# Attention context of a four-layer graph network: products of four heads in 32-column groups with denominators beside them, in place of 64-column products with a denominator column and transposes

## The chip, the cores and the metric

The kernel runs on one NeuronCore of one Trainium2 chip. The metric is the device time of one execution in microseconds (us). Before the change it is 3909.24 us, the median of two runs (3907.55 and 3910.94). Durations of single instructions come from one further execution under the profiler, which took 3906.41 us, with a span of 3904.6 us from its first to its last instruction.

## The reference

The reference takes 32 graphs of 512 nodes, each with 256 features (`x`, 32x512x256, fp32) and an adjacency matrix (`adj`, 32x512x512, int32). Four layers follow each other, and after each its output is added to its input and normalised. Layers 0, 1 and 3 are graph attention layers in which a neighbour's weight comes from two numbers per node. Layer 2 is a transformer layer with 8 heads of 32, and the part of it that matters here is this:

```python
allowed = (adj > 0) | (jnp.swapaxes(adj, 1, 2) > 0) | eye
qkv = x @ Wqkv.T + bqkv
scores = jnp.einsum('bhqd,bhkd->bhqk', q * scale, k)
scores = jnp.where(allowed[:, None], scores, -jnp.inf)
attn = jax.nn.softmax(scores, axis=-1)
ctx = jnp.einsum('bhqk,bhkd->bhqd', attn, v)
ctx = ctx.transpose(0, 2, 1, 3).reshape(B, N, DIM)
attn_out = ctx @ Wo.T + bo
x = _layernorm(x + attn_out, ln1_g, ln1_b)
ff = jax.nn.relu(x @ W1.T + b1) @ W2.T + b2
x = _layernorm(x + ff, ln2_g, ln2_b)
```

For each head, then, a context is a weighted sum of the rows of v, divided by the sum of the weights.

## The kernel before, in words

**Tiling.** A graph's 512 nodes are R = 4 tiles of 128 partitions, its 256 features K = 2 tiles. All work of a graph is in the function `fast_path`; a second function, `general_path`, runs only if a test of the inputs or of the denominators fails (`ok` and `sums` collect what the test needs), which it does not here.

**The order of the work.** `graph(b)` (L723) is a Python generator that writes down one graph's stages: the edge mask, layer 0, layer 1, the symmetric mask, `qkv`, `attention`, the projection (`attended`), `feed forward`, `layer 3`. Each stage is cut into units by `yield`. `paced` gives the unit after its i-th yield a due time, the graph's number times PERIOD plus an entry of the table PLACES, and `heapq.merge` interleaves the units of all 32 graphs by due time. A graph's work is some 430 us long in those units and the period is 120.5, so four graphs are in work at any time: attention of one lies between layer 1 of the next, the feed forward of the one before and so on. TensorE (PE) executes its instructions exactly in this order. The instructions of the other engines are ordered by the framework's scheduler, each in its own queue and in order within it; a helper, `in_place`, ties some of them to the last product before them. A wait of PE therefore holds up everything that is behind it, whichever graph it belongs to.

**PSUM.** There are 8 banks of 128x512 fp32. `bank` (L248) takes one for a product, from a set that depends on the stage: 2 for stages marked "a" (layers 0 and 1), 4 for "b" (qkv, attention, projection), 2 for "c" (feed forward, layer 3).

**qkv (L485).** The features are transposed (`xt2`), and q and k are formed for four heads at a time (qkp). ScalarE (ACT) takes a rounded copy `hi` out of PSUM, VectorE (DVE) the rest `lo`, and DMAs issued by SP spread them into a tile `qk` for two heads, from three buffers. Thus one product with reduced-precision operands gives a score of nearly full precision. v is kept for each node tile with 33 columns for a head: 32 values and a column of ones.

**Attention (L535).** Scores are computed transposed, keys on the partitions. For a pair of heads hp and a tile j of 128 keys there are two products s (128x512), two exponentials on ACT (L553, without subtraction of a maximum), and for j = 0 to 2 one multiplication by the mask on DVE (L556). For j = 3 the mask is instead added in PSUM by a second product with `shut`. When all four j of a pair are done, eight products `cp` follow, of 64 columns of v for each head: 32 values, the ones, and 31 columns of no interest. The two heads of a pair use the two halves of the array's columns and of one PSUM bank. ACT copies the bank to `cs` (L572). These eight products, of two instructions each because they are fp32, are one unit.

**Projection (L576).** The contexts stand with features on the partitions, but each head's denominator stands on one partition only. So for each node tile r four transposes (ctp<-cs) bring the nodes onto the partitions, a reciprocal (L587) and a multiplication (L591) divide, and eight further transposes (ctp<-ctx, in `transposed`, L306) turn the result back into `ct`, features on the partitions, as the product with Wo (wop) needs it.

What a PE unit is called later: s scores, cp context products, ctp context transposes, wop projection, f1p and f2p feed forward, o products of layers 0, 1 and 3, h0p, h1p, h3p their projections, gp a row of node numbers spread over partitions, xt0p to xt3p and ytp transposes.

Of the kernel before, what the change touches and what calls it, by code (L numbers as in the profile page):

```python
# [9 lines left out]
F32 = mybir.dt.float32  # L10
BF16 = mybir.dt.bfloat16
# [17 lines left out]
    "edges": [-1440, -1440, -410, 1420],  # L29
    "x": [3260],  # L30
    "mask": [16220, 16520, 16600, 17520],
    "layer 0": [
        2410, 3594, 4534, 4534, 5073, 5753, 5753, 5823, 6123, 6123, 6233, 6233, 6603, 6773, 6903,
        7687, 7687, 7777, 8077, 8077, 8157, 8287, 8439, 8439,
    ],
    "layer 1": [11037, 11066, 11277, 11729, 11849, 11879, 12043, 13286, 13554, 14195, 14884],
    "qkv": [17180, 17740, 18270, 18270, 18270, 18990, 19484, 19654, 21635, 21635],
    "attention": [
        20262, 20932, 21922, 21982, 22092, 22092, 22092, 22350, 22350, 23077, 23537, 23537,
        24028, 24208, 24328, 24532, 25064, 25220, 25368, 25943,  # L40
    ],
    "projection": [26801, 26801, 26861, 26911, 27661, 27721, 28721, 29140, 29256, 29848],
    "feed forward": [
        31013, 31120, 32042, 32263, 32263, 32465, 32710, 33771, 33983, 34076, 34284, 34691,
        35070, 35329, 35615, 36103, 36646, 37299,
    ],
    "layer 3": [39714, 39714, 40906, 41226, 41406, 41526, 41526, 42359, 42359, 42379, 42379],
# [6 lines left out]
RD_MAX = 1e25  # L54
# [18 lines left out]
def fast_path(ctx: ExitStack, tc: tile.TileContext, a: dict, out: bass.AP, bad: bass.AP):  # L73
# [21 lines left out]
    VC = DH + 1  # L95
    ND = R * (H + 2 + H2)
# [33 lines left out]
    sums = const.tile([P, 2, 2 * B], F32, name="sums")  # L130

# [4 lines left out]
    v = const.tile([P, R, H2 * VC + 2 * DH - VC], F32, name="v")  # L136
    nc.gpsimd.memset(v, 1.0)
# [110 lines left out]
    def bank(name, dtype=F32):  # L248
        shape = [P, 2048 // (2 if dtype == BF16 else 4)]
        n = 4 if stage[0] == "b" else 2  # L250
        return ps.tile(shape, dtype, tag="mm" + stage[0], name=name, bufs=n)

    def part(name):

        return buf([P, N], "part", name, {"a": 7, "b": 6, "c": 5}[stage[0]])
# [229 lines left out]
    def qkv(x):  # L485
# [31 lines left out]
        for r in range(R):  # L517
            yield
            p = bank("vp")
            for k in range(K):  # L520
# [7 lines left out]
            nc.scalar.copy(  # L528
                v[:, r, : H2 * VC].rearrange("p (h e) -> p h e", h=H2)[:, :, :DH],
                p[:, :D].rearrange("p (h e) -> p h e", h=H2),  # L530
            )
# [3 lines left out]
    def attention(qk, a2, shut):  # L535
        cs = []
        for hp in range(H2 // 2):
            pr = []
            for j in range(R):
                yield  # L540
                t = sb.tile([P, 2, N], F32, tag="pr", name="pr", bufs=4)
                for i in range(2):
                    s = bank("s")
                    product(nc.tensor.matmul,
                    s,
                        qk[hp][:, 1, i, j * P : (j + 1) * P],
                        qk[hp][:, 0, i, :],
                        start=True,
                        stop=j < R - 1,
                    )  # L550
                    if j == R - 1:
                        product(nc.tensor.matmul, s, identb, shut, start=False, stop=True)
                    nc.scalar.activation(t[:, i, :], s, AF.Exp, scale=QSCALE)  # L553
                if j < R - 1:
                    edges = a2[:, j, :].unsqueeze(1).to_broadcast([P, 2, N])
                    nc.vector.tensor_mul(t, t, edges)  # L556
                pr.append(t)

            yield
            cp = bank("cp")  # L560
            for j in range(R):
                for i in range(2):
                    first = (2 * hp + i) * VC
                    product(nc.tensor.matmul,
                    cp[i * 2 * DH : (i + 1) * 2 * DH, :],
                        v[:, j, first : first + 2 * DH],
                        pr[j][:, i, :],
                        start=j == 0,
                        stop=j == R - 1,
                    )  # L570
            t = part("cs")
            nc.scalar.copy(t, cp)  # L572
            cs.append(t)
        return cs

    def attended(x, cs, rd):  # L576
        ctx_ = []
        for r in range(R):
            yield
            p = bank("ctp")  # L580
            for hp in range(H2 // 2):
                product(nc.tensor.transpose,
                    p[:, hp * P : (hp + 1) * P], cs[hp][:, r * P : (r + 1) * P], ident
                )
            o = p.rearrange("p (h e) -> p h e", h=H2)
            rdr = rd[:, r * H2 : (r + 1) * H2].unsqueeze(2)
            nc.vector.reciprocal(rdr, o[:, :, DH : DH + 1])  # L587
            if r % 2 == 0:
                t = part("ctx").rearrange("p (r d) -> p r d", d=D)
            ctx_.append(t[:, r % 2, :])  # L590
            nc.vector.tensor_mul(  # L591
                ctx_[r].rearrange("p (h e) -> p h e", h=H2),
                o[:, :, :DH],
                rdr.to_broadcast([P, H2, DH]),
            )
# [805 lines left out]
```

## Time and profile before

| What | Value |
|---|---|
| median of the runs | 3909.24 us |
| the profiled execution | 3906.41 us |
| its span, first to last instruction | 3904.6 us |
| PE, matmuls: busy | 3753.3 us, 96% |
| DVE: busy | 2674.8 us, 69% |
| ACT: busy | 1926.2 us, 49% |
| GpSimd (POOL): busy | 346.9 us, 9% |
| DMA, main queue | 257.71 MB, 23.1% of 16 engines |
| mean granted TensorE clock | 0.983 |

In the lines of the profile, `L102 PE MATMUL cp<-pr,v 128*64 128x512 f32 x2048 | 474.9, 600 | 17.8 <-DVE ...` says: source line, engine, operation, tile written and tiles read, the array's rows and columns used, shape and type, count; then the busy time in us that is put down to the group and the mean of one in ns; then the idle time of the engine just before such instructions and what ended it. All products go through the helper `product`, so they all have line 102 and are told apart by their tiles. PEld is the weight load that goes with every matmul. Matmuls are pipelined, and their ends are modelled, so that durations overlap: the distance from one start to the next is the price of a matmul. In a timeline the first two columns are the start and the length of a run of like instructions. In a list of waits the columns after the colon are the total in us, the number of waits and the longest.

### The profile page before, as it was taken

The numbers are of one execution on the slowest core, as the hardware profiler recorded it, in microseconds if no ns is written. First come the engines' busy times: TensorE is split into PE (matmuls) and PEld (weight loads), VectorE is DVE, ScalarE is ACT, GpSimd is POOL, SyncE is SP. The second block draws the span as 40 slices with busy tenths as digits, with TensorE's granted clock in tenths as the row PEclk, the third lists the DMA queues.
The fourth block names the chain that finished last, engine by engine and source line by source line (L and its number), as shares of the span: only waits on it lengthen the run. The fifth ranks groups of instructions, "written<-read, shape, count | busy, mean of one in ns | idle before, by whom it ended". The sixth has DMA issues, their size and how long they took to land.

```text
span 3904.6 us, 53602 instructions
## 1 busy us (share of the span) xinstructions
PE 3753.3 (96%) x19238; PEld 2824.5 (72%) x19238; DVE 2674.8 (69%) x5594; ACT 1926.2 (49%) x4257; POOL 346.9 (9%) x266
## 2 busy tenths in 40 slices
PE   5899999999999999999999999999999999999996
PEld 4577777777777777777777777777777777777764
DVE  4667676677677677677677677677777677777653
ACT  2444455444455544455544455545555544555442
POOL 0000010000010001010001010001010001010000
PEclk6899999999999999999999999999999999999998
DMA  3222222222222222222222222222222222221120
GB/s 106 77 73 65 72 58 67 71 76 67 70 60 65 71 76 69 68 62 63 71 76 71 66 63 64 69 76 71 66 65 65 65 76 74 63 67 58 49 54 12
DMA packets 180431, 261.20 MB, mean 67 GB/s; under 512 B 36800, under 2 KB 72768, under 8 KB 180160
## 3 DMA queue, kind: packets, MB, share of 16 engines
q1 hardware_dynamic: 180160, 257.71, 23.1%
q8 instruction: 155, 2.54, 0.3%
q14 instruction: 116, 0.95, 0.1%
HBM read 106.57 MB, written 16.78 MB: 32 GB/s over the span
## 4 chain that ended last, share of the span: by engine, by line
PE 60%; DVE 14%; issue 8%; ACT 5%; POOL 5%; POOLq 0%; ACTq 0%
PE o L102 16%; PE f1p L102 7%; PE f2p L102 6%; PE qkp L102 5%; PE cp L102 5%; DVE pr L556 4%; ACT y L275 4%; POOL rs L270 3%; PE h3p L102 3%; PE s L102 3%; PE h1p L102 3%; PE wop L102 3%; POOL st L297 2%; PE gp L102 2%; PE vp L102 2%
## 5 line engine op out<-in xcount | busy, mean ns | idle before, releaser
L556 DVE TENSOR_TENSOR pr<-pr,a 128x1024 f32<-128x1024 f32 x384 | 459.1, 1216 | 319.3 <-ACT pr L553 319.2
L275 ACT ACTIVATE y<-y,rs 128x256 f32<-128x256 f32 x768 | 398.4, 589 | 438.2 <-DVE rs L271 438.2
L393 DVE SCALAR_TENSOR_TENSOR pt<-gb,ex,at 128x512 f32<-128x512 f32 x768 | 530.6, 744 | 77.6 <-ACT gb L345 77.6
L553 ACT ACTIVATE pr<-s 128x512 f32<-128x512 f32 x1024 | 545.2, 613 | 7.4 <-PE s L102 7.3
L102 PEld LDWEIGHTS o<-hv,pt 128*128 128x128 f32 x4096 | 508.4, 199 | 23.7 <-issue 8.4
L102 PE MATMUL o<-hv,pt 128*128 128x65 f32 x4096 | 502.7, 280 | 9.7 <-DVE pt L393 9.7
L102 PE MATMUL f2p<-wf,ft 128*128 128x256 f32 x2048 | 491.6, 383 | 12.3 <-ACT ft L638 12.2
L102 PE MATMUL cp<-pr,v 128*64 128x512 f32 x2048 | 474.9, 600 | 17.8 <-DVE pr L556 17.1
L102 PE MATMUL f1p<-yt,wf 128*128 128x256 f32 x2048 | 488.9, 381 | 0.3 <-DVE yt L302 0.3
L102 PE MATMUL o<-h,pt 128*128 128x257 f32 x2048 | 482.8, 383 | 3.7 <-DVE pt L393 3.7
L102 PEld LDWEIGHTS o<-h,pt 128*128 128x128 f32 x2048 | 381.5, 190 | 96.0 <-issue 40.6
L270 POOL TENSOR_TENSOR rs<-rs,mhalf 128x4 f32<-128x4 f32 x192 | 246.2, 1282 | 2118.8 <-DVE rs L269 1826.0
L638 ACT ACTIVATE ft<-f1p,cols 128x256 f32<-128x256 f32 x512 | 215.2, 474 | 442.2 <-PE f1p L102 442.2
L102 PEld LDWEIGHTS f2p<-wf,ft 128*128 128x128 f32 x2048 | 380.1, 191 | 69.5 <-ACT ft L638 17.1
L102 PEld LDWEIGHTS f1p<-yt,wf 128*128 128x128 f32 x2048 | 385.3, 191 | 54.5 <-DVE yt L302 0.8
L102 PE MATMUL s<-qk 128*128 128x512 f32 x1024 | 395.1, 481 | 1.6 <-ACT pr L553 1.6
L102 PEld LDWEIGHTS cp<-pr,v 128*64 128x64 f32 x2048 | 133.0, 136 | 286.0 <-issue 194.2
L266 DVE BATCH_NORM_STATS2 bn<-y 128x6 f32<-128x256 f32 x768 | 294.6, 411 | 4.5
L102 PEld LDWEIGHTS s<-qk 128*128 128x128 f32 x1024 | 187.8, 190 | 99.3 <-issue 40.6
L102 PE MATMUL qkp<-xt,wqkv 128*128 128x512 f32 x512 | 231.3, 594 | 0.0
L345 ACT COPY gb<-gp 128x512 f32<-128x512 f32 x192 | 111.5, 581 | 219.4 <-PE gp L102 219.4
L428 DVE RECIPROCAL rd<-o 128x4 f32<-128x4 f32 x128 | 23.4, 183 | 272.7 <-PE o L102 272.7
(134 smaller groups left out, 4582.5 us busy)
## 6 DMA issues: line engine op xcount, KB each, us to landing
qk<-hi SPq DMA_DIRECT2D x1024, 64.0 KB, 2.0
qk<-lo SPq DMA_DIRECT2D x1024, 64.0 KB, 2.0
adjt<-in_adjt SPq DMA_DIRECT2D x64, 512.0 KB, 3.5
adj<-in_adj SPq DMA_DIRECT2D x64, 512.0 KB, 3.6
xt<-in_xt SPq DMA_DIRECT2D x32, 512.0 KB, 3.4
x<-in_x SPq DMA_DIRECT2D x32, 512.0 KB, 4.7
out<-y SPq DMA_DIRECT2D x32, 512.0 KB, 3.0
wf<-in_w1t SPq DMA_DIRECT2D x1, 1024.0 KB, 7.6
```

The lines of the kernel that those rows point to most:

```text
L102: latest[0] = what(*args, **kwargs).ins.name
L266: nc.vector.bn_stats(st[:, r, :], y[:, r, :])
L270: nc.gpsimd.tensor_tensor(rs[:, 1, :], rs[:, 0, :], mhalf[:, :R], op=ALU.pow)
L275: nc.scalar.activation(y[:, r, :], y[:, r, :], AF.Identity, bias=rs[:, 2, r : r + 1], scale=rs[:, 1, r : r + 1],)
L297: nc.gpsimd.tensor_tensor(st[:, 2, :], st[:, 1, :], mhalf[:, :G], op=ALU.pow)
L345: nc.scalar.copy(g, p)
L393: nc.vector.scalar_tensor_tensor(t, g, f, edges, op0=ALU.max, op1=ALU.mult)
L428: nc.vector.reciprocal(rdh, o[:, :, HO:])
L553: nc.scalar.activation(t[:, i, :], s, AF.Exp, scale=QSCALE)
L556: nc.vector.tensor_mul(t, t, edges)
L638: nc.scalar.activation(ft[:, f, :], p[:, f, :], AF.Relu, bias=bf1[:, ff + f : ff + f + 1])
```

## The change

Layer 2's context products are arranged anew.

Attention now works on halves of the heads (c = 0 and 1, four heads each). For each tile j of keys the two pairs' scores, exponentials and masks come first, and then one unit of eight products: four `cp`, of 32 columns of v for each of the four heads, into one PSUM bank, each head in its own quarter of the array's columns and of the partitions; and four `dp`, the same with a constant 128x32 tile of ones in place of v, into another bank. So every partition of a head holds that head's denominator. The two banks accumulate over the four j, and there are two such banks in all (tag acc).

At the end of a half, DVE forms the reciprocal of dp (128x512) and multiplies cp by it straight into `ct`, which has the features on the partitions already. Two sums on ACT for each half (over dp and over rec) feed the test at the end of the kernel in place of the small reciprocals that `ok` held before. The copies `cs`, all ctp transposes, the small reciprocals, the divisions and the copies out of PSUM into `ct` are gone. v has 32 columns a head, and is copied flat.

Further: the products of stages a and b share one set of four banks; there are five buffers for probabilities in place of four, and two of the tag part in stage b in place of six; and the table PLACES has new due times for all stages, with the same period. The end of the kernel has some more instructions on small tiles.

```diff
-    VC = DH + 1
-    ND = R * (H + 2 + H2)
+    ND = R * (H + 2)
...
-    sums = const.tile([P, 2, 2 * B], F32, name="sums")
+    sums = const.tile([P, 4, 2 * B], F32, name="sums")
...
-    v = const.tile([P, R, H2 * VC + 2 * DH - VC], F32, name="v")
-    nc.gpsimd.memset(v, 1.0)
+    v = const.tile([P, R, D], F32, name="v")
+    ones = const.tile([P, DH], F32, name="ones")
+    nc.gpsimd.memset(ones, 1.0)
...
-        n = 4 if stage[0] == "b" else 2
-        return ps.tile(shape, dtype, tag="mm" + stage[0], name=name, bufs=n)
+        tag, n = ("c", 2) if stage[0] == "c" else ("ab", 4)
+        return ps.tile(shape, dtype, tag="mm" + tag, name=name, bufs=n)
...
-            nc.scalar.copy(
-                v[:, r, : H2 * VC].rearrange("p (h e) -> p h e", h=H2)[:, :, :DH],
-                p[:, :D].rearrange("p (h e) -> p h e", h=H2),
-            )
+            nc.scalar.copy(v[:, r, :], p[:, :D])
...
-    def attention(qk, a2, shut):
-        cs = []
-        for hp in range(H2 // 2):
-            pr = []
+    def attention(b, qk, a2, shut):
+        ct = sb.tile([P, K, N], F32, tag="ct", name="ct", bufs=1)
+        for c in range(K):
+            acc = [ps.tile([P, N], F32, tag="acc", name=n, bufs=2) for n in ("cp", "dp")]
             for j in range(R):
+                pr = []
+                for hp in range(2):
+                    yield
+                    t = sb.tile([P, 2, N], F32, tag="pr", name="pr", bufs=5)
+                    for i in range(2):
+                        s = bank("s")
+                        product(nc.tensor.matmul,
+                            s,
+                            qk[2 * c + hp][:, 1, i, j * P : (j + 1) * P],
+                            qk[2 * c + hp][:, 0, i, :],
+                            start=True,
+                            stop=j < R - 1,
+                        )
+                        if j == R - 1:
+                            product(nc.tensor.matmul, s, identb, shut, start=False, stop=True)
+                        nc.scalar.activation(t[:, i, :], s, AF.Exp, scale=QSCALE)
+                    if j < R - 1:
+                        edges = a2[:, j, :].unsqueeze(1).to_broadcast([P, 2, N])
+                        nc.vector.tensor_mul(t, t, edges)
+                    pr += [t[:, 0, :], t[:, 1, :]]
                 yield
...
-            yield
-            cp = bank("cp")
-            for j in range(R):
-                for i in range(2):
-                    first = (2 * hp + i) * VC
-                    product(nc.tensor.matmul,
-                    cp[i * 2 * DH : (i + 1) * 2 * DH, :],
-                        v[:, j, first : first + 2 * DH],
-                        pr[j][:, i, :],
-                        start=j == 0,
-                        stop=j == R - 1,
-                    )
-            t = part("cs")
-            nc.scalar.copy(t, cp)
-            cs.append(t)
-        return cs
+                for o, p in enumerate(acc):
+                    for i in range(4):
+                        first = (4 * c + i) * DH
+                        product(nc.tensor.matmul,
+                            p[i * DH : (i + 1) * DH, :],
+                            ones if o else v[:, j, first : first + DH],
+                            pr[i],
+                            start=j == 0,
+                            stop=j == R - 1,
+                        )
+            rec = part("rec")
+            nc.vector.reciprocal(rec, acc[1])
+            nc.vector.tensor_mul(ct[:, c, :], acc[0], rec)
+            for o, t in enumerate((acc[1], rec)):
+                junk = sb.tile([P, N], BF16, tag="junk", name="junk", bufs=1)
+                i = 2 * b + c
+                nc.scalar.activation(junk, t, AF.Copy, accum_out=sums[:, 2 + o, i : i + 1])
+        return ct
...
-            p = bank("ctp")
-            for hp in range(H2 // 2):
-                product(nc.tensor.transpose,
-                    p[:, hp * P : (hp + 1) * P], cs[hp][:, r * P : (r + 1) * P], ident
-                )
...
-            nc.vector.reciprocal(rdr, o[:, :, DH : DH + 1])
...
-        ct = yield from transposed(ctx_, "ct")
```

Of PLACES, the rows that touch attention (in hundredths of a us, by the table's own clock):

```diff
     "attention": [
-        20262, 20932, 21922, 21982, 22092, 22092, 22092, 22350, 22350, 23077, 23537, 23537,
-        24028, 24208, 24328, 24532, 25064, 25220, 25368, 25943,
+        20222, 20892, 22312, 22312, 22312, 22702, 22702, 22702, 23260, 23260, 23260, 23837,
+        24057, 24127, 24502, 24502, 24502, 24872, 25302, 25444, 26080, 26580, 26580, 26880,
     ],
-    "projection": [26801, 26801, 26861, 26911, 27661, 27721, 28721, 29140, 29256, 29848],
+    "projection": [29111, 29590, 29906, 29928],
```

## The prediction

> **What bounds the kernel now.** I read the page's busy shares first, then the busy times of two neighbouring stretches in the middle of the run, then what TensorE waited for there, then the groups, then the timeline around the lines that change. The page:
>
> ```profile
> PE 3753.3 (96%) x19238; PEld 2824.5 (72%) x19238; DVE 2674.8 (69%) x5594; ACT 1926.2 (49%) x4257; POOL 346.9 (9%) x266
> PE   5899999999999999999999999999999999999996
> ```
>
> TensorE is full from the third slice to the last but one. A busy PE is a modelled figure, so I look at the rhythm. The chain in order of time has the layer 3 transposes (xt3p x5) at 1952.60 and again at 2069.35 us: one graph every 116.75 us. Two stretches of that length, by engine (PE, PEld, DVE, ACT, POOL):
>
> ```profile
> 2000.00:2116.78 116.78, 115.09 (x602) 86.99 (x601) 83.12 (x175) 60.01 (x133) 10.75 (x8) 1.00 0.24 68
> 2116.78:2233.56 116.78, 115.08 (x602) 86.98 (x601) 83.11 (x175) 60.01 (x133) 10.76 (x8) 1.00 0.24 68
> ```
>
> They are alike to 0.01 us: a steady state at full clock, in which TensorE is idle for 116.78 - 115.09 = 1.69 us. What it waits for, over 20 graphs (1000 to 3336 us):
>
> ```profile
> PE gp L102 <- ACT ex L665: 14.1, 20, 0.7
> PE cp L102 <- DVE pr L556: 9.9, 20, 0.5
> PE xt3p L102 <- ACT y L275: 9.8, 60, 0.2
> ```
>
> These are 0.70, 0.49 and 0.49 us for each graph, the whole 1.69. So the period is the sum of what TensorE is given, and a microsecond per graph, taken or added, is about 32 us of the total. The groups that change:
>
> ```profile
> L102 PE MATMUL cp<-pr,v 128*64 128x512 f32 x2048 | 474.9, 600 | 17.8 <-DVE pr L556 17.1 <-DVE mv L267 0.6
> L102 PE MATMUL ctp<-ident,cs 128*128 128x128 f32 x512 | 67.2, 279 | 2.7 <-ACT cs L572 2.7
> L102 PE MATMUL ctp<-ident,ctx 128*128 128x128 f32 x256 | 39.5, 280 | 0.0
> L591 DVE TENSOR_TENSOR ctx<-ctp,rd 128x256 f32<-128x256 f32 x128 | 48.4, 418 | 0.0
> L587 DVE RECIPROCAL rd<-ctp 128x8 f32<-128x8 f32 x128 | 17.7, 178 | 0.0
> ```
>
> The means of PE overlap, so I take prices from starts. One visit of the context products (16 instructions: each fp32 product is two), in the timeline of PE:
>
> ```profile
> 2055.94 1.90 PE L102 MATMUL o<-h,pt 128*128 128x257 f32 x8
> 2057.77 3.65 PE L102 MATMUL cp<-pr,v 128*64 128x512 f32 x16
> 2061.35 0.48 PE L102 MATMUL o<-h,pt 128*128 128x257 f32 x1
> ```
>
> From start to next start a visit takes 3.58 us, and the o before it 1.83 where eight such instructions otherwise take 1.73: 3.68 in all. Single weight loads of the visit begin in pairs 0.43 us apart: the two column halves run side by side, 8 pairs x 0.43 = 3.43, and 0.25 goes on entering and leaving. And the way from scores to masked probabilities, PE, ACT and DVE in one timeline:
>
> ```profile
> 2035.65 1.27 PE L102 MATMUL s<-qk 128*128 128x512 f32 x4
> ...
> 2036.33 2.06 ACT L553 ACTIVATE pr<-s 128x512 f32<-128x512 f32 x4
> ...
> 2036.76 1.89 PE L102 MATMUL f1p<-yt,wf 128*128 128x256 f32 x8
> 2037.45 2.36 DVE L556 TENSOR_TENSOR pr<-pr,a 128x1024 f32<-128x1024 f32 x2 [3.31 <-ACT pr L553]
> ```
>
> Four scores occupy PE for 1.11 us, but the second masked pair is ready only at 2039.81, 4.16 us after the first score began, with ACT and DVE both free for it.
>
> **What the skill says.** "TensorE: Matmul & The Clock Gate", Part 3 (packing small matmuls), has matmuls in different column groups running at once, three of 32 columns 2.38 times as fast as one after the other. The trace agrees for two halves; four are not shown. "TensorEngine Tiling (Array Packing)", Key Properties, has a change of the tiling mode drain the array; the 0.25 us per visit agrees. "VectorE: DVE Perf Modes", on the fixed hardware budget, has the reciprocal iterate with a repeat count of 8. The trace has only small ones: 128x1 in 154 to 162 ns, 128x8 in 178, some 2 to 3 ns per element.
>
> **The change part by part, per graph.**
>
> 1. *Transposes gone.* 16 + 8 of ctp; four of them take 0.44 us in the chain (1953.36 to 1953.80): 6 x 0.44 = -2.6 us of PE. With them go four evacuations cs (0.58 each, ACT), ct (0.66 DVE, 0.60 ACT), four small reciprocals (0.18) and four divisions (0.42): 3.1 us of DVE, 2.9 of ACT, all off the path.
>
> 2. *Products.* Four visits of 8 matmuls become eight visits of 8 (4 cp, 4 dp), again 16 instructions each, now in four column groups. If all four run at once a visit takes 4 x 0.43 + 0.25 = 1.97. 8 x 1.97 - 4 x 3.68 = +1.0 us. Lower bound: as stated, since array time is already shared out fully; upper bound under the rivals.
>
> 3. *Old waits.* In the order that the built program gives the engines, two wop units now stand between the last h3p and the gp of layer 3, xt3p comes later behind the feed forward that it needs (some 15.2 us of PE work after the last f2p, 14.4 were needed), and a cp no longer waits as before. -1.7 us at most; I take it and book new waits below.
>
> 4. *New sure waits.* Before, a visit came after all four j of a head pair, so that all but its last probabilities were old. Now a visit needs the four tiles of its own j, and TensorE's order is fixed: everything queued behind it waits. In two of eight visits (first half of the heads j=0, second half j=1) only four scores and one feed forward unit stand ahead: 1.11 + 1.73 + 0.1 of entry = 2.95 us, against 4.16. With j=0 the scores of that place took 1.4, so 1.1 and 1.2: +2.3 us. Both have the DVE first pair ready at about the arrival; what lacks is the second.
>
> 5. *New likely waits*, from laying the new DVE and ACT order out with durations of before. f2p of j=1 waits for ft behind four exponentials: 0.3. The visit j=1, first half: DVE has two 1.2 us additions between its two masks and behind GpSimd's 2.9 us power: 0.4. The fourth qk tile gets its buffer only when the first half's last scores are read (three buffers, two now in use at a time); its 16 DMAs are issued by SP 0.63 apart and land 2.0 later, 11.5 us, against some 11.1 of PE work: 0.4; adj and xt loads queue behind and have tens of us. Visit j=0, second half: both sums over dp and rec stand between two exponentials on ACT: 0.45. gp of layer 3: the four normalisations of layer 1 now stand before h3's last copy on ACT: 0.8. o3: DVE writes its pt after bn and wop additions: 0.65. Together 3.0; each hangs on chains of ten steps that I can place to about a microsecond, so I take 1.8 and keep 0 to 3.0.
>
> 6. *Reciprocals.* Two of 128x512. From below 0.68 us (128x512 f32 out of PSUM on DVE, as y<-f2p 684 ns), from above 512 x 8 / 0.96 GHz, an estimate from the skill's repeat count with the clock that page gives: 4.3. By the slope of the small ones 1.2 to 1.7; I take 2.5. DVE then has 83.1 - 3.1 + 2 x 2.5 + 2 x 0.68 = 86.4 us per graph, no bound. The first half's has 6 us until its acc banks are used again, the second's 7 until wop: hidden up to about 3 us; at 4.3 it delays the masks and gp behind it, +1.8. The four ACT sums (0.6 each) replace evacuations of equal length; beyond the place named they are covered by ACT's half idle time.
>
> 7. *Edits together at no cost:* flat v copy, no memset of v, smaller rd and ok, the three DVE instructions each that end the check (some 0.2 us each, once: +1 us at the end, lost in rounding). Banks of stages a and b are shared, 4 in place of 2 + 4; in the attention stretch every bank comes free before its turn by my layout. Startup and tail have slack; +-5 us.
>
> Sum: -2.6 + 1.0 - 1.7 + 2.3 + 1.8 = +0.8 us per graph, x 32 = +26. The profiled execution took 3906.4 (span 3904.6); the median of the runs is 2.8 above it. 3906.4 + 26 + 2.8 = 3935 us.
>
> **Rivals.**
>
> *Four groups don't run side by side* (the slower end). Place: every product visit. If only pairs overlap, a visit keeps 3.68 us: 8 x 1.71 = 13.7 us more, +438: 4373. For it: no line shows more than two. Against: pairs lose nothing at all (0.43 for two, and 0.43 is what qkp, 128x512 at full width, takes for one). It decides from 0.48 us for a quad: 8 x 4 x 0.054 = 1.7 us, which carries the sum past 2%.
>
> *The order hides all of step 5.* Before, the order leaves 1.7 us per graph idle, so such orders can be tight. -2.6 + 1.0 - 1.7 + 2.3 = -1.0: 3877.
>
> *Long reciprocals, all of step 5 real.* -2.6 + 1.0 - 1.7 + 2.3 + 3.0 + 1.8 = +3.8, +122: 4031. For it: DVE has no gap in the stretch of attention but the one for GpSimd.
>
> That the transposes stay is excluded: the built program has none of ctp.
>
> **How the numbers follow.** Forecast 0.48 (3900 to 3980), hidden 0.25, long reciprocals 0.17, no fourfold overlap 0.10. From 3870 to 4030 leaves out about 0.05 below and most of the last rival above with part of the third. About 2%, 78 us, is what a measurement of this kernel can tell from no change: faster by more needs -2.4 us per graph, beyond what is left with the sure waits, 0.04. Slower by more (over 3987): 0.10, half of the third rival 0.08, a tail of the forecast 0.02: 0.20.
>
> **What will show it.** Right: cp and dp visits of about 2.0 us where they don't wait; a period near 117.6; PE waits of cp on DVE pr of about 2.3 us per graph in two visits; ctp gone and nothing in its place. Wrong: weight loads of a visit that begin two by two 0.43 apart (first rival); cp hardly waiting (the exponentials overtaken in a way I missed); rec at over 3 us with waits behind it; or an engine order in which waits for banks appear in layers 0 and qkv, where I laid out least.

## The result

The changed kernel takes **4201.56 us** (median of two runs, 4199.16 and 4203.96), against 3909.24 before: a ratio of 1.0748, 95% interval 1.0702 to 1.0794. The prediction was 3935 us with a range up to 4030, so it was wrong, and on the slow side. The profiled execution's span is 4197.3 us, against 3904.6. Its page has TensorE less full:

```profile
PE 3906.6 (93%) x20454; PEld 2775.9 (66%) x20518; DVE 2836.2 (68%) x5440; ACT 1955.6 (47%) x4353; POOL 409.6 (10%) x266
...
PE   5799999999999999999999999999999999999986
```

A period (from the first wop of a graph to the first of the next) was 116.75 to 116.79 us before. Now it is 125.26 on average (graphs 8 to 28), mostly of two kinds. One of each, and a stretch inside the first (columns as before; the last three are the TensorE clock, the DMA share and GB/s):

```profile
1725.86:1853.89 128.03, 122.76 (x639) 88.48 (x640) 88.24 (x170) 60.87 (x138) 13.05 (x8) 0.96 0.22 62
1977.56:2101.19 123.63, 118.33 (x640) 84.01 (x641) 87.95 (x170) 60.99 (x138) 13.05 (x8) 1.00 0.23 65
...
1737.65:1746.83 9.18, 9.18 (x41) 8.81 (x42) 7.68 (x23) 1.48 (x3) 1.36 (x1) 0.50 0.13 36
```

Most graphs take 123.6 us; about one in three takes some 4.3 more, because TensorE's clock stands at 0.50 for 10.2 us. That happens 8 times between 600 and 3500 us, and twice more for 3.4 us; before, half clock was seen only at the two ends of the run. What TensorE waited for, over 20 graphs (1000 to 3500 us, the total, the number and the longest):

```profile
PE gp L101 <- ACT ex L649: 40.0, 20, 2.0
PE vp L101 <- ACT gb L344: 13.5, 20, 0.7
PE f2p L101 <- ACT ft L622: 11.3, 20, 0.6
PE s L101 <- DMA qk<-lo: 9.5, 7, 2.0
PE s L101 <- ACT pr L553: 9.2, 12, 1.0
PE s L101 <- ACT exp L476: 9.0, 20, 0.5
PE o L101 <- ACT xt L303: 4.5, 16, 0.3
PE cp L101 <- DVE pr L556: 3.7, 20, 0.2
```

These are 5.0 us a graph; two smaller lines, 0.2 us together, are left out. The waits inside the product visits are not in this list, since some of a visit's products go ahead of those that wait. The timeline of PE shows them: a visit that doesn't find its probabilities ready (the first four lines, 3.0 us to the end of the last, the runs of cp and dp broken up), and one that does (the last two lines; the s after them begins 1.85 us after the first cp):

```profile
2077.11 1.76 PE L101 MATMUL cp<-pr,v 128*32 128x512 f32 x6
2078.25 0.62 PE L101 MATMUL dp<-pr,ones 128*32 128x512 f32 x2
2078.69 0.60 PE L101 MATMUL cp<-pr,v 128*32 128x512 f32 x2
2078.71 1.44 PE L101 MATMUL dp<-pr,ones 128*32 128x512 f32 x6
...
2086.41 1.06 PE L101 MATMUL cp<-pr,v 128*32 128x512 f32 x8
2087.29 1.04 PE L101 MATMUL dp<-pr,ones 128*32 128x512 f32 x8
```

Four of the eight visits wait, 1.37 + 1.20 + 0.95 + 0.92 = 4.4 us in a graph, from the distances between starts less those of a ready visit. TensorE's idle time in a graph at full clock is 123.63 - 118.33 = 5.3 us. With the visits' 4.4, of which 0.4 are in that idle time already, it waits some 9.3 us a graph; before it was 1.69. The new groups:

```profile
L571 DVE RECIPROCAL rec<-dp 128x512 f32<-128x512 f32 x64 | 214.7, 3354 | 128.2 <-PE dp L101 128.2
...
L101 PE MATMUL cp<-pr,v 128*32 128x512 f32 x2048 | 403.3, 611 | 32.5 <-DVE pr L556 26.7
...
L101 PE MATMUL dp<-pr,ones 128*32 128x512 f32 x2048 | 379.1, 600 | 0.0
```

So the products themselves are cheap and side by side. 123.6 less 9.3 leaves 114.3 us of work for TensorE, against 116.77 - 1.69 = 115.08 before. The change saved 0.8 us of work, and lost more than ten times as much in waits and in the clock that follows them. The experiments ask why: is it the work that the change added (column groups on TensorE, the 3.35 us reciprocal on DVE), or the order in which the queues serve TensorE?

### The profile page after: what moved, and what is told of

It is laid out like the page before. It is cut to its first block, busy times and chain, and to the rows that moved or that the text cites. A ratio compares the mean times of both kernels' runs of the same rounds, so it can differ in the third digit from the quotient of the medians.

```text
span 4197.3 us, 55888 instructions
## 1 busy us (share of the span) xinstructions
PE 3906.6 (93%) x20454; PEld 2775.9 (66%) x20518; DVE 2836.2 (68%) x5440; ACT 1955.6 (47%) x4353; POOL 409.6 (10%) x266
## 4 chain that ended last, share of the span: by engine, by line
PE 52%; DVE 25%; ACT 5%; POOL 4%; SPq 3%; issue 2%; DMA 1%; POOLq 0%; DVEq 0%; ACTq 0%
PE o L101 13%; PE f2p L101 8%; PE f1p L101 7%; PE cp L101 5%; PE qkp L101 5%; DVE pr L556 4%; POOL rs L269 4%; PE s L101 4%; PE dp L101 4%; SPq L511 3%; DVE bn L265 3%; DVE rec L571 2%; DVE pt L392 2%; ACT y L274 2%; PE h1p L101 2%
## 5 line engine op out<-in xcount | busy, mean ns | idle before, releaser
L101 PEld LDWEIGHTS o<-hv,pt 128*128 128x128 f32 x4096 | 537.7, 208 | 41.1 <-ACT xt L303 14.0
L101 PE MATMUL o<-hv,pt 128*128 128x65 f32 x4096 | 542.0, 290 | 17.1 <-DVE pt L392 10.5
L101 PE MATMUL o<-h,pt 128*128 128x257 f32 x2048 | 503.0, 392 | 12.1 <-DVE pt L392 11.9
L269 POOL TENSOR_TENSOR rs<-rs,mhalf 128x4 f32<-128x4 f32 x192 | 284.4, 1481 | 2188.7 <-DVE rs L268 2138.3
L101 PE MATMUL cp<-pr,v 128*32 128x512 f32 x2048 | 403.3, 611 | 32.5 <-DVE pr L556 26.7
L101 PE MATMUL dp<-pr,ones 128*32 128x512 f32 x2048 | 379.1, 600 | 0.0
L571 DVE RECIPROCAL rec<-dp 128x512 f32<-128x512 f32 x64 | 214.7, 3354 | 128.2 <-PE dp L101 128.2
```

Source lines behind the costliest of these rows:

```text
L101: latest[0] = what(*args, **kwargs).ins.name
L269: nc.gpsimd.tensor_tensor(rs[:, 1, :], rs[:, 0, :], mhalf[:, :R], op=ALU.pow)
L571: nc.vector.reciprocal(rec, acc[1])
```

## The experiments

In the first four, the edited kernel was left to the scheduler, which put DVE and ScalarE into a new order each time. In the later ones, but for TensorE's places alone, that order is held, by dependencies between neighbours that do nothing but order. The periods are means over graphs 8 to 28, between first wops.

| Kernel | us | ratio to before, 95% | period |
|---|---|---|---|
| before | 3909 | | 116.77 |
| after | 4201.56 | 1.0702 to 1.0794 | 125.26 |
| short reciprocal, order left free | 4167.68 | 1.0631 to 1.0693 | 124.42 |
| h3 earlier | 4249.92 | 1.0841 to 1.0904 | 126.89 |
| late products | 4128.34 | 1.0531 to 1.0592 | 123.82 |
| before, gp made late | 4188.49 | 1.0684 to 1.0746 | 126.29 |
| short reciprocal, order held | 4137.66 | 1.0562 to 1.0605 | 123.29 |
| gp first, order held | 4172.65 | 1.0643 to 1.0705 | 124.13 |
| after, order of need | 4150.34 | 1.0595 to 1.0637 | 123.69 |
| late products, order of need | 4039.82 | 1.0318 to 1.0352 | 120.69 |
| before, order of need | 3878.23 | 0.9905 to 0.9938 | 115.89 |
| after's work, new order | **3807.93** | 0.9725 to 0.9751 | 113.31 |
| the same, TensorE's places alone | 4168.16 | 1.0640 to 1.0679 | 125.45 |
| before, new order | 3851.93 | 0.9834 to 0.9867 | 114.44 |

### Short reciprocal, order left free

```diff
-            nc.vector.reciprocal(rec, acc[1])
+            nc.vector.tensor_copy(rec, acc[1])
```

The division is left out.

> The changed kernel with the two reciprocals of 128x512 (3.35 us each on VectorE) replaced by copies of dp out of PSUM (an estimated 0.7 us); what is left out is the division, so contexts are multiplied by their denominators. My theory after the trace: two separate losses. (a) Half of the product visits wait for masks because they stand too close behind their scores in TensorE's order and because the masks queue behind layer normalisation steps on VectorE; the reciprocals have no part in it. (b) The second reciprocal of a graph pushes the normalisation of layer 1, that lies ahead of the last copy of h3 on ScalarE, and so gp waits 2.2 us; after that wait TensorE's clock is halved for 9 us in about one graph of three. So only (b) goes: gp 2.2, the wait behind it 0.3, clock 1.5, together 3 to 4 us per graph: about 4075 to 4105 us, with the product visits' waits still at about 4.4 us per graph. Rival 'VectorE is overloaded': with 5.3 us less of work per graph the visits' waits shrink too, by 2 us or more: below 4030. Rival 'the half clock belongs to the four column groups': the half clock stays, 4120 to 4130. Rival 'reciprocals are hidden': 4190 to 4202.

It gained 34 us, a third of the least that was expected. gp's wait fell to 0.6 us, and with it the half clock went from the middle of the run but for two stretches of 3.4 us; but o now waited 1.0 us for DVE's pt, and graphs at full clock still took 123.9. A confounded run, though: the scheduler had put both queues into another order.

### h3 earlier

```diff
-    "layer 3": [40934, 40934, 41196, 41196, 41496, 41916, 42046, 42679, 42779, 42799, 43059],
+    "layer 3": [40934, 40934, 41196, 41196, 41496, 41496, 42046, 42679, 42779, 42799, 43059],
```

> The changed kernel with one due time different: the fourth h3 product of layer 3 at 41496 in place of 41916, ahead of the second wop, so that ScalarE copies it before the normalisation of layer 1 comes to it. My theory: gp finds its ex and doesn't wait (2.2 us per graph less, and 0.3 behind it), and the half clock goes with the wait (1.5 less): 3 to 4 us per graph, about 4075 to 4105 us, though the reciprocals are as long as before. Rival 'the second reciprocal holds up more than gp' : the wait moves to another user of VectorE or ScalarE (xt2p, o), and the gain is below 1 us per graph: above 4170. Rival 'the half clock belongs to the four column groups': the wait goes and the half clock stays: 4115 to 4130.

gp's wait went, and three others came in its place (xt2p for xt 0.7, o for y 0.6, xt2p for y 0.3 us a graph): graphs at full clock take 123.9 us, no less than in after, and half clock is now in most graphs. 48 us slower.

### Late products

The products of key tile j are written down behind the scores of j+1, and so asked for later:

```diff
-            for j in range(R):
-                pr = []
-                for hp in range(2):
+            pr = {}
+            for j in range(R + 1):
+                for hp in range(2 * (j < R)):
...
-                            ones if o else v[:, j, first : first + DH],
-                            pr[i],
+                            ones if o else v[:, j - 1, first : first + DH],
+                            pr[j - 1][i],
```

with due times of attention to match.

> The changed kernel with each product unit (cp and dp of a j) written after the scores of the next j, with due times to match: mostly one or two feed forward units of 1.7 us more between scores and products. My theory: the waits inside the product visits, 4.4 us per graph, fall below 1 us: 3.4 to 4.4 us per graph less, about 4060 to 4095 us, gp and the half clock as they were. Rival 'VectorE is overloaded': the masks are late wherever the products stand, the waits fall by less than 2 us per graph: above 4140. Rival 'the visits are long by themselves, the four column groups do not run at once if the order on the engine is unfavourable': visits stay at 2.3 to 2.5 us from first to last start: above 4180.

It is 73 us faster, where 107 to 142 were expected. All the waits of the visits are gone, 4.4 us, but the period is only 1.4 us shorter. From its list of waits:

```profile
PE f2p L101 <- ACT ft L624: 79.8, 41, 3.3
PE o L101 <- DVE pt L392: 20.7, 21, 1.0
PE s L101 <- ACT exp L476: 20.4, 20, 1.0
```

f2p, which had waited 0.6 us, now waits 4.0 a graph. So the visits look like the place where a late queue showed, not like what made it late; the scheduler's new order and the moved due times are in this run too, and keep it from being proof.

### Before, with gp made late

Two idle copies on ScalarE ahead of the exponentials that gp of layer 3 needs, in the kernel before:

```diff
+        for _ in range(2):
+            nc.scalar.copy(h[:, 1:, :], h[:, 1:, :])
```

> The kernel before with two in-place copies of three quarters of h3 (128x774 each, an estimated 0.8 us) on ScalarE ahead of ex, so that gp of layer 3 waits about 2.3 us where it waited 0.7; nothing else is changed and no product of four column groups is in it. My theory, that the wait alone brings the half clock: 1.6 us per graph for the wait and 1 to 2 for stretches of half clock in about one graph of three: 3980 to 4025 us. Rival 'the half clock belongs to the four column groups': the wait alone, 3955 to 3965 us, mean clock as before at 0.983.

Some 1.7 us of ScalarE's work made the kernel before 279 us slower, where 71 to 116 were expected: a period of 126.29 in place of 116.77. Its two main waits:

```profile
PE f2p L102 <- ACT ft L638: 75.1, 20, 3.8
PE gp L102 <- ACT ex L667: 48.8, 20, 2.4
```

f2p waits 3.8 us and gp 2.4 in each graph. The waits of before that are gone taken off, that is 5.0 us more waiting, and two stretches at half clock (6.8 and 3.4 us long) make up the other 4.5. f2p's wait was not expected: the scheduler's order has changed here too. No column group of 32, no long reciprocal is in it. Waits like after's, and the clock's answer to them, are thus to be had without any of the new work.

### Short reciprocal, order held

The edit of the first run, with DVE and ScalarE held in exactly the order of after.

> The changed kernel with the order of DVE and ScalarE held exactly as it was, and the reciprocal replaced by a copy of the same 128x512 tile (the division is left out); unlike e1, where the scheduler put both queues in another order, this is one change. If the second reciprocal is what makes gp late (a DVE queue without gaps behind it: it ends about 2.5 us sooner), gp's wait of 2.0 us goes, and the half clock behind it: 121.5 us a period, 4070 to 4110. If another chain sets gp's time and the reciprocal only sits beside it: 4140 to 4200, gp still waiting over 1.2 us.

64 us faster, a little over half of what the first case expected and just past the edge of the second. A graph at full clock, and two of the waits:

```profile
1951.09:2074.10 123.01, 118.17 (x640) 84.07 (x640) 82.96 (x170) 60.80 (x137) 13.05 (x8) 1.00 0.23 65
```

```profile
PE gp L343 <- ACT ex L891: 31.0, 20, 1.6
PE vp L343 <- ACT gb L586: 13.5, 20, 0.7
```

gp still waits 1.55 us, over the 1.2 that the second case named: the two long reciprocals themselves are worth 0.6 us a graph, and another 1.4 because the half clock is gone between 600 and 3500 us. The rest of gp's lateness has another cause.

### gp first, order held

After, with one edit to ScalarE's order: the last copy h<-h3p and layer 3's ex go ahead of layer 1's four normalisations y<-y,rs, behind which they had stood. In after's timeline of ScalarE (the third line waits for the first two):

```profile
2108.27 2.08 ACT L274 ACTIVATE y<-y,rs 128x256 f32<-128x256 f32 x4 [2.22 <-DVE rs L270]
2110.25 0.35 ACT L332 COPY h<-h3p 128x258 f32<-128x258 f32 x1
2110.64 0.21 ACT L649 ACTIVATE ex<-h 128x4 f32<-128x4 f32 x1
```

> The changed kernel with the order of DVE and ScalarE held as it was but for one edit a graph: the last copy h<-h3p and the three small ex instructions of layer 3 go ahead of the four normalisations y<-y,rs of layer 1 that they stood behind, where ScalarE was idle for 2.2 us. If gp's wait of 2.0 us was the price of that place (as step 5 booked it), it is gone, and the half clock with it: 121.5 to 122 us a period, 4065 to 4100. Rival, that the place is only where a later limit shows: the transposes xt2p right behind gp need those same normalised rows, which are as late as before, so PE waits there nearly as long and the time is the same, 4150 to 4205.

The rival was right on the period. gp doesn't wait any more, and the transposes behind it and the products behind those do:

```profile
PE o L343 <- DVE pt L634: 18.4, 18, 1.0
...
PE xt2p L343 <- DVE y L838: 10.9, 20, 0.6
...
PE xt2p L343 <- ACT y L516: 6.5, 40, 0.2
```

Graphs at full clock take 123.54 us, as in after. But gp's idle time, now in smaller pieces, brings the half clock less often (three stretches of 3.4 to 6.8 us from 600 to 3500 us, in place of after's ten), and that alone is the 29 us gained. So gp was only the first in TensorE's order to need something from behind the normalisation of layer 1. Why that is late can be read in after's timelines of DVE and of GpSimd:

```profile
2096.16 3.35 DVE L571 RECIPROCAL rec<-dp 128x512 f32<-128x512 f32 x1
...
2105.88 0.15 DVE L268 SCALAR_TENSOR_TENSOR rs<-mv 128x4 f32<-128x4 f32 x1
2105.95 1.22 DVE L409 TENSOR_TENSOR hv<-hv 128x1024 f32<-128x1024 f32 x1
```

```profile
2106.11 1.92 POOL L269 TENSOR_TENSOR rs<-rs,mhalf 128x4 f32<-128x4 f32 x1 [10.06 <-DVE rs L268]
```

From the reciprocal on DVE works without a gap until 2107.2; only at 2105.9 does it come to the rs of layer 1. GpSimd's power then takes 1.92 us where it takes 1.01 at 2095.04, and ends 0.86 us after the multiplication that DVE began just before it.

### The order of need

No instruction is added or taken away. Of the next four instructions in the queue of DVE, and likewise of ScalarE, the one goes first whose result TensorE needs first, worked out backwards from TensorE's order with durations of the traces:

```diff
+        for engine, places in ORDER.items():
+            row = [names[engine][k] for k in places]
+            for one, two in zip(row, row[1:]):
+                tc.add_manual_dep(by_name[two], one, only, reason="held")
```

Applied to after, to the late products, and to before:

> The changed kernel with its own places for TensorE's work, and DVE and ScalarE held in the order of need as in o1; nothing else. 'Order, not work' splits in two here: if DVE's and ScalarE's order is the whole of it, this is near before, 3920 to 4000; if TensorE's own places matter too (products asked for right behind their last score), adding up gives about 119 + 3 = 122 us a period, 4050 to 4110, with the waits of the products for their probabilities and of layer 3's transposes left over. Rival 'the work costs it': 4150 to 4200.

> Late products as in e3, and in addition the DVE and ScalarE instructions are held in another order by dependencies that only order them: of the next four in the old order, the one whose result TensorE needs first goes first (the need worked out backwards from TensorE's own order with the durations of the traces); the first two graphs keep the old order. Not one instruction is added, removed or changed. Theory 'order, not work' (the instructions that the change put in are paid for by those that it took out; the loss is that DVE and ScalarE serve TensorE in the wrong order): adding those durations up by this order gives a period about 6.5 us below after's and 0.8 above before's, so 117 to 119 us, 3920 to 4000 in all. Rival 'the four-column products and the long reciprocals cost it themselves' (TensorE interrupted by column groups, DVE by 3.35 us instructions): no order helps much, 4080 to 4130, as e3. Rival 'the half clock': as long as waits near 2 us remain, over 4050.

> Control: the kernel before, with DVE and ScalarE held in the order of need by the same rule. If the rule as such makes kernels faster, before gains as well, 3800 to 3880, and o1 proves nothing on the change. If before's order was already as good as the rule makes it, adding up gives a period 0.8 us longer, 3900 to 3950.

The late products gained 88 us by it and end below what either rival allowed, though not at 3920 to 4000 as "order, not work" had it; after gained 51 and stands at the edge of the rival that blames the work. So order counts, and neither case had the size. What I had left out of the adding up is an order that the instructions themselves impose. The late products' list of waits:

```profile
PE f2p L348 <- ACT ft L871: 36.5, 21, 2.0
PE h1p L348 <- ACT h L579: 33.5, 21, 1.6
PE vp L348 <- ACT gb L591: 25.7, 20, 1.3
PE s L348 <- ACT exp L723: 16.3, 21, 0.8
```

h1p, for one, waits for a copy that stands behind the sum over dp on ScalarE, and that sum in turn waits until DVE's 3.35 us reciprocal over the same bank has ended, though it doesn't read the reciprocal. The Trainium skill, "PSUM — Partial Sum Buffer", section "PSUM bank collisions raise a hardware error", says that the compiler's scheduler puts a dependency between instructions of different engines that touch the same bank and partitions, even where both only read. The trace agrees that there is one here, once a graph, from ScalarE's list of waits:

```profile
ACT junk L826 <- DVE rec L820: 38.8, 21, 1.9
```

Control: before gained 31 us, a period 0.9 us shorter, where 0.8 longer was added up. By its own expectation that is the case in which the rule makes kernels faster as such. So the 88 us of the late products can't be read as a loss that the change brought; only some 57 of them are more than before gained by the same rule.

### A new order altogether

Again after's work and nothing else (products of j behind the scores of j+1), with that bank dependency in the sum, new due times for TensorE, and the order of need among the next six. Both were chosen together so as to leave little waiting. Its attention row, with line breaks set for comparison:

```diff
-        20222, 20892, 22312, 22312, 22312, 22702, 22702, 22702, 23260, 23260, 23260, 23837,
-        24057, 24127, 24502, 24502, 24502, 24872, 25302, 25444, 26080, 26580, 26580, 26880,
+        18437, 18437, 22312, 22579, 23083, 23083, 23083, 23083, 23083, 23083, 23083, 23089,
+        23491, 24554, 24604, 24812, 24888, 24888, 24888, 24894, 24897, 25453, 25456, 25456,
```

> The work of the changed kernel (the products of j written down behind the scores of j+1, as in e3), with new due times for TensorE's units throughout and DVE and ScalarE held in the order of TensorE's need (of the next six in the old order, the one needed first). No instruction is added, removed or changed; both orders were chosen together by adding up durations of the traces, so that little waiting is left (gp 0.7 us a graph, f2p 0.3). Theory 'order, not work': TensorE has been given 114.6 us a graph in o1 once its waits are taken off, some of it the entries and exits of units, so a period of 112 to 115 us, and 3780 to 3860 in all, faster than before. Rival 'four-column products and long reciprocals cost it': 4000 to 4100, as no order of o1, e3 or oa came below 4039. The half clock stays away from steady graphs in the first case.

**3807.93 us, 2.6% faster than before**, as the theory had it. One wait is left, and two graphs in a row are alike:

```profile
PE gp L327 <- ACT ex L632: 10.0, 22, 0.5
```

```profile
1920.72:2034.03 113.31, 112.62 (x640) 83.58 (x640) 88.58 (x170) 60.29 (x136) 10.77 (x8) 1.00 0.25 70
2034.03:2147.33 113.30, 112.59 (x640) 83.59 (x640) 88.49 (x170) 60.29 (x136) 10.77 (x8) 1.00 0.25 70
```

The same 640 matmuls as in after, the same reciprocals, in 12 us less. That rules out the work itself as the cause of after's loss. GpSimd's busy time is 10.8 us again, against 13.05.

> The same kernel and due times as o2, but DVE's and ScalarE's order left to the scheduler, which knows nothing of TensorE's needs. If TensorE's own order were what matters, near o2. If it takes both (a TensorE order is only as good as the two queues that feed it): adding up gives about 10 us a graph more than o2, 4080 to 4250, with TensorE waiting in new places.

With the same due times but DVE and ScalarE left to the scheduler: 4168.16, as the second case had it. cp waits for pr again (2.4 us a graph), h3p 3.2, o 1.9. Neither order alone comes near 3808: TensorE's places give 4168, DVE's and ScalarE's 4150 with after's places (after, order of need) and 4040 with the late products.

### The control

The kernel before, with a new order made in the same way:

> Control for o2: the kernel before (64-column products, transposes and all) with new due times and DVE and ScalarE held in the order of need, both chosen by the same adding up and with as much search as for o2. If o2's gain was only the new order and the change itself is worth nothing, this is as fast as o2, 3800 to 3820. If the change saves TensorE about 1.6 us a graph as steps 1 and 2 had it, this one ends 1.5 to 2 us a graph above o2's 113.3: 114.7 to 115.3 a period (before without its three waits is 115.1), 3850 to 3875.

```profile
2057.07:2171.50 114.43, 113.84 (x602) 86.88 (x601) 84.19 (x175) 60.41 (x133) 10.91 (x9) 1.00 0.24 69
```

3851.93 us, period 114.44: 1.13 us a graph above the change in its new order, where 1.5 to 2 were expected. So of the 102 us by which the new-ordered change beats before, some 58 are to be had without the change, and 44 us, 1.1%, are left to it. The runs of the two kernels lie far apart (3805 to 3809, 3850 to 3853), but each stands for the best order that one search found; that both searches were equally good isn't shown.

## Why the prediction was wrong

Per graph, in us:

| Term | predicted | measured |
|---|---|---|
| steps 1 and 2, transposes gone, products in four groups | -1.6 | -0.8 |
| step 3, old waits gone | -1.7 | -1.7 |
| step 4, sure waits of two visits | +2.3 | +2.6 |
| step 5, likely waits | +1.8 | +6.7 |
| not in the list: half clock | 0 | +1.7 |
| sum | +0.8 | +8.5 |

The 31 periods from the first wop to the last grew by 264 us in all, of the 292.7 by which the span grew; the first wop came 21.9 us later, and the end after the last one took 6.3 longer. Step 7 had allowed 5 for that. I didn't look into it.

*Step 1 was right*: no ctp, nothing in its place. *Step 2 was right in kind*: the weight loads of a visit begin four at a time, 7 ns apart, in rounds of 0.43 us, so that a ready visit takes 1.95 us with its entry and exit, where 1.97 was predicted. The first rival is dead. The two steps together are 0.8 less work by the balance above, and 1.2 by TensorE's busy time in the two kernels with new orders (112.6 and 113.84), not 1.6. The distances between starts in these two traces show where the rest went: the transposes were worth 2.6 us and the products cost 0.4 more, but the other units take 1.0 us more, most of it f2p, s and f1p. What entering a visit costs is part of that; the rest stays open. *Step 3*: the three waits of before went as stated; what gp waits for now is booked in step 5. *Step 4 was right*: 1.37 and 1.20 for 1.1 and 1.2. (The 1.1 has some luck in it: 1.4 + 1.73 + 0.1 against 4.16 leaves 0.9.)

*Step 5 is the step that failed.* Piece by piece: f2p 0.6 (0.3 predicted), first half j=1 0.95 (0.4), the scores behind the fourth qk tile and their own bank 0.9 (0.4), gp 2.0 (0.8), o3's pt 0.1 (0.65), second half j=0 nothing (0.45); and not foreseen at all, first half j=2 0.9, vp 0.7, s behind the exponentials of layer 1 0.45, o behind xt 0.2. The last s reads nothing of layer 1's, so that what it waits for can only be a bank of the set that stages a and b now share: step 7's "every bank comes free before its turn" was wrong there. A kernel that differs in this alone was not tried. I put the error down to one root, which is a reading of the traces and not shown piece by piece. I laid the new queues out with the durations of before and looked at each place by itself, took a wait for the price of its place, and then took 60% of the list on the ground that each was uncertain. They were not independent: in the chain in order of time, about 38 us of a graph run from a score of the second half through ScalarE, DVE and GpSimd before TensorE is on it again, and a chain that is late shows wherever TensorE next needs it. That fits "late products", "h3 earlier" and "gp first": each removed its waits, and the period at full clock hardly moved. What is shown is the cause as a whole: the same work in another order of all three queues has none of these waits but 0.5 of gp. The opposite hope (the rival in which the order hides step 5) wasn't wrong about the work: the new order is that case and more, since it hides step 4 too, at 3808 for 3877. The order that came with the change is not that order.

*The half clock was in no step.* The timeline of PE in the slow graph of above, and two stretches of the same place:

```profile
1735.56 0.65 PE L101 MATMUL gp<-ident,ex 128*128 128x128 f32 x4 [2.00 <-ACT ex L649]
1736.05 1.05 PE L101 MATMUL xt2p<-ident,y 128*128 128x128 f32 x8
1737.38 7.09 PE L101 MATMUL o<-hv,pt 128*128 128x65 f32 x32 [0.27 <-ACT xt L303]
```

```profile
1733.52:1736.93 3.41, 1.41 (x13) 1.28 (x12) 3.41 (x6) 2.88 (x10) 0.00 (x0) 1.00 0.00 0
1736.93:1747.17 10.24, 9.97 (x43) 9.42 (x42) 8.74 (x25) 2.21 (x5) 1.36 (x1) 0.50 0.15 46
```

32 products o take 7.09 us there, 3.79 where the clock is full. So gp's wait of 2.0 us had a price beyond itself; with 1.55 (short reciprocal, order held) it had none. But the length of one wait isn't the measure. In "h3 earlier" waits of 0.7 and 0.6 us close together were enough:

```profile
1116.74:1120.15 3.41, 2.06 (x17) 1.73 (x16) 3.41 (x9) 0.76 (x2) 0.00 (x0) 1.00 0.00 0
1120.15:1126.98 6.83, 6.83 (x31) 6.55 (x30) 5.93 (x18) 1.32 (x3) 1.36 (x1) 0.50 0.03 7
```

As the period before had no wait over 0.7, its profile could not show this.

*Step 6* mis-sized one term: the reciprocal takes 3.35 us where I took 2.5, between its bounds. The first one lies hidden, as said: the visit behind it doesn't wait. The second was said to be hidden up to 3 us; the two together cost 0.6 a graph by themselves, and 2.0 with the clock. The third rival had this mechanism, at 4031; it fell short for the same reason as the forecast, that its waits were step 5's.

## What to carry to other kernels

Where one engine is nearly full and its order is fixed, a change that frees it of work can still lose many times as much by asking for results sooner than the other queues give them; count the chain through the other engines, not each wait, since a wait that is taken away at one place comes up at the next. Try such a change together with an order of all queues made for it, and give the old kernel the same care before you say what the change is worth. Read the row of the clock beside the waits: 1.3 to 2 us of idle time close together brought half clock here, in some places though not in others.

## What the runs showed of the hardware

- **Half clock after a short idle time.** In each of the fourteen traces the clock changes only at points 3.41 us apart, and all stretches of half clock between 600 and 3500 us last 3.4, 6.8 or 10.2 us. In after there are ten of them. Each follows an interval of this grid in which TensorE was idle for 1.87 to 2.01 us, and no interval without one behind it had more than 1.91. A wait of 2.0 us falls whole into one interval in (3.41 - 2.0) / 3.41 = 0.4 of all cases, an estimate from these figures that fits the one graph in three. Idle time alone isn't the rule: 1.35 us was enough in "h3 earlier", and 1.55 in each graph wasn't with the short reciprocals. What else counts stays open. The Trainium skill, "TensorE: Matmul & The Clock Gate", Part 1, has a freely running window of about 3.4 us, half clock after at least one idle window and full clock after at least one busy one. The grid agrees with such a window; but here no window was idle throughout, and coming back mostly took three such intervals.
- **GpSimd waits for DVE.** Its power rs takes 1.0 us, but ends 0.86 us after a DVE instruction with two inputs that began before it (1.92 us above). The skill's "SBUF — State Buffer", section "SBUF: two separate sides", says that such a DVE instruction locks out a GpSimd one that reads SBUF until its end; the trace agrees. It cost 2.3 us of GpSimd's time a graph (13.05 against 10.8). It isn't what made after slow: the late products have 10.3 us, and still 122.9 a period at full clock.
- **Four column groups of fp32 products** start 7 ns apart, and a round of four takes 0.43 us, as long as one product of 128x512 over all columns takes (qkp): no loss by packing within a visit.
- **A reciprocal of 128x512** fp32 out of PSUM takes 3.35 us, 6.5 ns for an element of a partition, against the 2 to 3 that the small ones had suggested.
